# Layer 1's output mix applied to 128 middle features, and layers 1 and 2 skewed by a block in shared pools

## The chip, the cores and the metric

The kernel runs on one core of a Trainium2 chip, all in fp32. Its five engines work side by side, each in the order of its own instruction list: TensorE (PE in the profile, with its weight loads as PEld), VectorE (DVE), ScalarE (ACT), GpSimd (POOL), and SyncE (SP), which here only issues DMAs. The metric is the device time of one execution in microseconds; lower is better.

## The reference

Four graph layers over x of 128 x 64 x 256 (batch, node, feature), each in the form x = x + layer(relu(layernorm(x))):

```python
# layer 0: mix with a normalised adjacency, linear, batch norm, relu, linear, batch norm
# layer 1: spectral; U are the eigenvectors of the normalised Laplacian of adj
agg = jnp.einsum('mn,bnd->bmd', U.T, features)      # 256 features
h = jax.nn.relu(agg @ W1 + b1)                      # 128 features
out = h @ W2 + b2                                   # 256 features
return jnp.einsum('nm,bmd->bnd', U, out)
# layer 2: two adjacency layers, then LSTMs over windows of 1 to 4 nodes
h = jax.nn.relu(jnp.einsum('ts,bsh->bth', adj, x @ Wg0 + bg0))
h = jax.nn.relu(jnp.einsum('ts,bsh->bth', adj, h @ Wg1 + bg1))
...
# layer 3: edge attention over 512 edges
```

The eigenvectors U are computed on the chip, from a tridiagonal form made by Householder steps.

## The kernel before

The rows (128 x 64 = 8192) are cut into NB = 16 blocks of BT = 512 rows; a block X[i] is a resident tile of 128 partitions x TPB = 4 x D = 256. Two graphs of 64 nodes share the 128 partitions, so a mix over nodes is a matmul with a 128 x 128 block-diagonal matrix: BDU and BDUT for U and its transpose, BDA for the adjacency.

The program has these stages in order. `eigenvectors` computes U together with layer 0: a planner (`Plan`) lays layer 0's matmuls between the steps of the eigenvector chain and writes the order out by hand. A value is then loaded into a register and a branch (`self.tc.If`) holds a slower eigenvector method for the case that the fast one fails. `block_diagonal` makes BDA, BDU and BDUT after the branch. `layer1` follows, then `adjacency_layers`, the LSTM `windows`, and `layer3`. Outside the planned part the order on each engine is that of a scheduler that fills in by priority and readiness.

`layer1` for block i: `end0` (ACT applies layer 0's last batch norm to the stored `big` tiles, TensorE transposes them, VectorE adds them to X), `norm` (bn_stats, bn_aggr and a square root by steps, tiles n_st, n_mv, n_v, n_y, n_r, n_m; then ACT writes `h`), `mix` with BDU into `a`, W1 into PSUM, ACT's ReLU with bias b1 into `z`, W2 into PSUM, VectorE's addition of b2 into `y`, BDUT on y, and VectorE's addition to X. `adjacency_layers` first makes its tables (row sums w2_rs, B0, N0, b1) from ones, AT and the biases, then for each block runs norm, mix with BDA, W0, a max with the table N0 (`g`), W1, addition of b1 (`y`), and a second mix whose ReLU goes to `big` through ACT. In block 2 it also makes layer 3's tables from the list of edges (`edges`), in PSUM buffers of its own. Each of the two layers has pools of its own, opened with waits on what was in their place before.

DMAs go out on SP's queue in program order: the two adjacencies, 16 loads of X, layer 0's weights, the small vectors, then the rows of the Householder steps (`f_V<-f_x`, line 1046). Layer 1's weights are loaded inside `layer1`, after the branch, and layer 2's inside `adjacency_layers`.

Every matmul, VectorE and ACT instruction is recorded through one helper (`Ordered.call`), so all of them have line L799 in the profile and are told apart by their tiles; TensorE's `ps<-a,w` is W1 of layer 1 or W0 of layer 2, `pt<-w,z` or `pt<-z,w` is W2, `pt<-y,BDUT` the output mix, `pt<-ident,big` end0's transposes.

Of the kernel before, what the change touches and what calls it, by code (L numbers as in the profile page):

```python
# [8 lines left out]
F32 = mybir.dt.float32  # L9
# [885 lines left out]
class Fast:  # L895
# [197 lines left out]
    def reflectors(self):  # L1093
# [16 lines left out]
        for k in range(6):  # L1110
            p = self.mm((NT[:], B[:]))
            B2 = t(f"B{k + 1}", 64, 64)
            o.tt(B2[:], B[:], p[:], ALU.add if k else ALU.subtract)
            B = B2
            if k < 5:
                N2, NT2 = t(f"N{k + 1}", 64, 64), t(f"NT{k + 1}", 64, 64)
                self.act(N2[:], self.mm((NT[:], N[:]))[:], AF.Copy)
                self.act(NT2[:], self.mm((N[:], NT[:]))[:], AF.Copy)
                N, NT = N2, NT2
# [70 lines left out]
    def values(self):  # L1190
# [35 lines left out]
        X1 = t("X1", 128, 64)  # L1226
# [4 lines left out]
        F = t("F", 64, 64)  # L1231
# [124 lines left out]
    def verdict(self, U):  # L1356
# [4 lines left out]
        row, r2 = t("k_row", 64, 64), t("k_r2", 64, 64)  # L1361
# [63 lines left out]
P = 128  # L1425
# [21 lines left out]
class Kernel:  # L1447
# [57 lines left out]
    def block_diagonal(self, name, M, psum):  # L1505

        nc = self.nc
        bd = self.c(name, P, P)
        nc.vector.memset(bd[:], 0.0)
        p = psum.tile([P, N], F32, name="adj_ps")  # L1510
        self.mm(p[:], self.I2[:], M)
        self.o.copy(bd[0:64, 0:64], p[0:64, :])
        self.o.copy(bd[64:128, 64:128], p[64:128, :])
        return bd

    def adjacency(self, fast, plan):
# [9 lines left out]
        self.BDH = self.c("BDH", P, P)  # L1526
        nc.vector.memset(self.BDH[:], 0.0)
        rs, cs, dg, deg, junk = t("rs", 1), t("cs", 1), t("dg", 1), t("deg", 2), t("junk", N)
# [50 lines left out]
    def eigenvectors(self):  # L1579
# [3 lines left out]
        with ExitStack() as ex:  # L1583
# [12 lines left out]
            plan.emit()  # L1596
            bad = nc.values_load(left[0:1, 0:1], min_val=0, max_val=64)
# [5 lines left out]
        with ExitStack() as cx:  # L1603
            psum = cx.enter_context(self.tc.tile_pool(name="adjps", bufs=2, space=PSUM))
            self.BDA = self.block_diagonal("BDA", self.AT[:], psum)
            self.BDU = self.block_diagonal("BDU", self.U[:], psum)
            self.BDUT = self.block_diagonal("BDUT", self.UT[:], psum)
# [10 lines left out]
    def norm(self, pool, i, h=None):  # L1618
# [3 lines left out]
        if h is None:  # L1622
            h = pool.tile([P, TPB, D], F32, name="h")
        st = pool.tile([P, TPB, 6], F32, name="n_st")
        mv = pool.tile([P, TPB, 2], F32, name="n_mv")
        v, r, m = (pool.tile([P, TPB], F32, name="n_" + x) for x in "vrm")
# [5 lines left out]
        self.rsqrt(pool, r[:], v[:], "n")  # L1632
        o.stt(m[:], mv[:, :, 0], -1.0, r[:], ALU.mult, ALU.mult)
        for j in range(TPB):
            self.act(h[:, j, :], X[:, j, :], AF.Relu, scale=r[:, j:j + 1], bias=m[:, j:j + 1])
# [253 lines left out]
    def end0(self, i, psum):  # L1889

        sc2, sh2 = self.affine2
        for oc in range(2):
            self.act(self.part(i, oc), self.part(i, oc), AF.Identity, scale=sc2[:, oc:oc + 1], bias=sh2[:, oc:oc + 1])
        self.add_transposed(psum, i, lambda dc, j: self.part(i, dc)[:, j * P:(j + 1) * P])
# [3 lines left out]
    def layer1(self):  # L1898
        o, io = self.o, self.io
        cx, (w, pool, psum, ps2, ps0) = self.stage([("l1w", 1), ("l1", 2), ("l1ps", 3), ("l1bps", 3), ("l1eps", 2)])  # L1900
        with cx:
            W1 = self.weights(w, "w1_1", io["L1_gnn_W1"])
            W2 = self.weights(w, "w1_2", io["L1_gnn_W2"])
            b1 = self.columns(w, "w1_b1", io["L1_gnn_b1"])
            b2 = self.everywhere(w, "w1_b2", io["L1_gnn_b2"])

            self.end0(0, ps0)
            self.end0(1, ps0)
            hs = {0: self.norm(pool, 0)}
            for i in range(NB):  # L1910
                if i + 2 < NB:
                    self.end0(i + 2, ps0)
                if i + 1 < NB:
                    hs[i + 1] = self.norm(pool, i + 1)
                h = hs.pop(i)
                a = pool.tile([P, 2, BT], F32, name="a")
                self.mix(psum, h, self.BDU, lambda dc, p: self.move(a[:, dc, :], p[:]))
                p = psum.tile([P, BT], F32, name="ps")
                for kc in range(2):
                    self.mm(p[:], W1[:, kc, :], a[:, kc, :], kc == 0, kc == 1)  # L1920
                z = pool.tile([P, BT], F32, name="z")
                self.act(z[:], p[:], AF.Relu, bias=b1[:, 0:1])
                for jj in range(0, TPB, 2):
                    p = ps2.tile([P, 2, D], F32, name="pt")
                    for j in range(2):
                        self.mm(p[:, j, :], z[:, (jj + j) * P:(jj + j + 1) * P], W2[:, 0, :])
                    y = pool.tile([P, 2, D], F32, name="y")
                    o.add(y[:], p[:], b2[:, None, :].to_broadcast([P, 2, D]))
                    p = ps2.tile([P, 2, D], F32, name="pt")
                    self.mm(p[:].rearrange("p a b -> p (a b)"), self.BDUT[:], y[:].rearrange("p a b -> p (a b)"))  # L1930
                    x = self.X[i][:, jj:jj + 2, :]
                    o.add(x, x, p[:])
# [3 lines left out]
    def layer2(self):  # L1936
        self.adjacency_layers()
        self.windows()

    def adjacency_layers(self):  # L1940
        nc, o, io = self.nc, self.o, self.io
        cx, (w, pool, psum, ps2) = self.stage([("l2w", 1), ("l2", 2), ("l2ps", 4), ("l2bps", 2)])
        with cx:
            W0 = self.weights(w, "w2_0", io["L2_gnn_Wg0"])
            W1 = self.weights(w, "w2_1", io["L2_gnn_Wg1"])
            b0 = w.tile([1, D], F32, name="w2_b0")
            nc.sync.dma_start(b0[:], io["L2_gnn_bg0"][None, :])
            b1 = self.everywhere(w, "w2_b1", io["L2_gnn_bg1"])


            rs = w.tile([1, P], F32, name="w2_rs")
# [4 lines left out]
            B0, N0 = w.tile([P, 2, P], F32, name="w2_B"), w.tile([P, 2, N], F32, name="w2_N")  # L1956
# [9 lines left out]
            for i in range(NB):  # L1966
                if i == 2:
                    with ExitStack() as ce:
                        epool = ce.enter_context(self.tc.tile_pool(name="l3e", bufs=1, side="right"))
                        epsum = ce.enter_context(self.tc.tile_pool(name="l3eps", bufs=1, space=PSUM))  # L1970
                        nc.vector.hold, nc.scalar.hold, nc.tensor.hold = nc.vector.last, nc.scalar.last, nc.tensor.last
                        self.edges(self.w3, epool, epsum)
                        nc.vector.hold = nc.scalar.hold = nc.tensor.hold = None
                h = self.norm(pool, i)
                nc.sync.dma_start(self.spilled(i), self.X[i][:])
                a = pool.tile([P, 2, BT], F32, name="a")
                self.mix(psum, h, self.BDA, lambda dc, p: self.move(a[:, dc, :], p[:]))
                g = pool.tile([P, 2, BT], F32, name="g")
                for hc in range(2):
                    p = psum.tile([P, BT], F32, name="ps")  # L1980
                    for kc in range(2):
                        self.mm(p[:], W0[:, kc, hc * P:(hc + 1) * P], a[:, kc, :], kc == 0, kc == 1)
                    o.tt(g[:, hc, :].rearrange("p (b n) -> p b n", n=N), p[:].rearrange("p (b n) -> p b n", n=N),
                         N0[:, hc, None, :].to_broadcast([P, BT // N, N]), ALU.max)
                y = pool.tile([P, TPB, D], F32, name="y")
                for jj in range(0, TPB, 2):
                    p = ps2.tile([P, 2, D], F32, name="pt")
                    for j in range(2):
                        for kc in range(2):
                            self.mm(p[:, j, :], g[:, kc, (jj + j) * P:(jj + j + 1) * P], W1[:, kc, :],  # L1990
                                    kc == 0, kc == 1)
                    o.add(y[:, jj:jj + 2, :], p[:], b1[:, None, :].to_broadcast([P, 2, D]))
                v = self.nodes(i // 4)
                b = 8 * (i % 4)
                self.mix(psum, y, self.BDA, lambda dc, p: self.act(
                    v[:, dc, :, b:b + 8].rearrange("p n b -> p b n"), p[:].rearrange("p (b n) -> p b n", n=N), AF.Relu))
# [188 lines left out]
    def edges(self, w, pool, psum):  # L2185
# [28 lines left out]
        ps = [psum.tile([P, E], F32, name=f"ps{x}") for x in range(2)]  # L2214
# [12 lines left out]
        self.OS, self.OD = (pool.tile([P, E], F32, name="ed_" + n) for n in ("OS", "OD"))  # L2227
# [5 lines left out]
        for a, y in ((self.OS, self.OST), (self.OD, self.ODT)):  # L2233
            p = psum.tile([P, 4, N], F32, name="ps0")
# [10 lines left out]
        p = psum.tile([P, E], F32, name="ps1")  # L2245
# [3 lines left out]
        p = psum.tile([P, E], F32, name="ps0")  # L2249
# [201 lines left out]
    def run(self):  # L2451
# [4 lines left out]
        with cx:  # L2456
            self.big = [pool.tile([P, 2, 4 * BT], F32, name="big") for pool in pools]
            self.eigenvectors()
            self.layer1()
# [46 lines left out]
```

## Time and profile before

| | before |
|---|---|
| median of 3 runs | 2392.77 us (2391.76 to 2393.52) |
| profiled execution | 2392.81 us, of which the span is 2391.0 |
| mean granted TensorE clock | 0.989 |
| layer 0 and eigenvectors | 0 to about 382 us |
| branch | 382 to 388.9 us |
| layer 1 | 388.9 to 532.7 us |
| adjacency layers of layer 2 | 532.7 to 730.9 us |
| LSTM windows, then layer 3 | 730.9 to the end |

The profile gives, for each engine, the time that it was busy; a matmul in fp32 appears as two records. Records of TensorE overlap (their ends are modelled), so the distance between starts, and not the duration, is what one costs in a row. A window's row gives the busy time of PE, PEld, DVE, ACT and POOL in a stretch, each with its count, then the granted clock, the share of the DMA engines and what they moved. In a timeline or a group, the bracket or the last column is the idle time before the instruction and what ended it.

### The profile page before, as it was taken

The page shows a single profiled execution, that of the slowest core. Times are in us where ns is not written, and L with a number is a line of the kernel's source. Part 1 is how long each engine was busy: PE and PEld are TensorE (multiplying, and loading weights), DVE is VectorE, ACT ScalarE, POOL GpSimd, SP SyncE. Part 2 cuts the span into 40 slices and gives each one's busy share as a digit, 9 for nine tenths or more (in the row PEclk, how much of TensorE's full clock was granted, in tenths as well). Part 3 has the DMA queues.
Part 4 walks back from the last instruction along what each step waited for, and adds up shares of the span by engine and source line. Part 5 has one row for each costly group of instructions (what it writes and reads, how often), then busy time and mean ns, then how long its engine had stood idle before and what let it go on. Part 6 is the DMA issues. An engine that isn't in the chain of part 4 may idle for free.

```text
span 2391.0 us, 31925 instructions
## 1 busy us (share of the span) xinstructions
PE 2306.4 (96%) x11801; PEld 1601.0 (67%) x11801; DVE 1601.8 (67%) x4044; ACT 1137.3 (48%) x2488; POOL 2.5 (0%) x23
## 2 busy tenths in 40 slices
PE   5997998989999999999999999999999999999989
PEld 3554444656777778888999999888884444444434
DVE  6887675877536776677776677559755565656467
ACT  4675767434435663444444444335536544434321
POOL 0000000000000000000000000000000000000000
PEclk9999998999999999999999999999999999999989
DMA  5000211221001000000100002000011000000001
GB/s 159 1 1 1 71 54 33 69 82 36 1 1 36 1 18 1 1 1 1 36 1 1 1 1 71 1 1 16 1 34 38 1 5 18 14 14 18 14 14 49
DMA packets 61048, 54.77 MB, mean 23 GB/s; under 512 B 15188, under 2 KB 58709, under 8 KB 60885
## 3 DMA queue, kind: packets, MB, share of 16 engines
q1 hardware_dynamic: 60884, 52.66, 7.1%
q8 instruction: 95, 1.56, 0.3%
q14 instruction: 69, 0.56, 0.1%
HBM read 35.86 MB, written 16.78 MB: 22 GB/s over the span
## 4 chain that ended last, share of the span: by engine, by line
PE 78%; DVE 4%; ACT 1%; issue 1%; ACTq 0%; DVEq 0%
PE ps L799 67%; PE pt L799 5%; PE acc L799 5%; DVE sm_m L799 1%; PE y L799 1%; DVE X L799 1%; DVE aw L799 0%; DVE n_st L799 0%; ACT ls_g L799 0%; DVE g L799 0%; ACT big L799 0%; DVE sm_e L799 0%; DVE ls_g L799 0%; DVE y L799 0%; DVE n_mv L799 0%
## 5 line engine op out<-in xcount | busy, mean ns | idle before, releaser
L799 ACT ACTIVATE ls_g<-ls_g,ls_b 128x512 f32<-128x512 f32 (+4 forms) x472 | 243.0, 565 | 154.6 <-DVE ls_g L799 152.8
L799 ACT ACTIVATE ls_g<-ps,ls_b 128x256 f32<-128x256 f32 (+3 forms) x268 | 115.4, 470 | 329.4 <-PE ps L799 325.4
L799 PE MATMUL ps<-z,w 128*128 128x512 f32 x512 | 255.6, 625 | 0.0
L799 PE MATMUL ps<-big,X 128*128 128x176 f32 (+3 forms) x848 | 212.8, 366 | 1.1 <-ACT ls_z L799 1.0
L799 DVE TENSOR_TENSOR aw<-at,ed_OST 128x1024 f32<-128x1024 f32 x128 | 149.9, 1220 | 92.2 <-PE ps L799 92.2
L799 DVE TENSOR_TENSOR ls_g<-ls_z,ps 128x512 f32<-128x512 f32 (+5 forms) x256 | 146.9, 579 | 91.5 <-PE ps L799 90.0
L799 PE MATMUL ps<-ls_tx,X 128*128 128x160 f32 (+2 forms) x960 | 206.7, 326 | 1.2 <-DVE X L799 0.6
L799 PE MATMUL ps<-X,X 128*128 128x160 f32 (+1 forms) x896 | 199.0, 306 | 0.0
L799 PE MATMUL ps<-X,ls_w 128*128 128x256 f32 x640 | 190.5, 379 | 0.0
L799 PEld LDWEIGHTS ps<-ls_tx,X 128*128 128x128 f32 x960 | 161.8, 190 | 15.9 <-DVE X L799 5.5
L799 PEld LDWEIGHTS ps<-big,X 128*128 128x128 f32 x848 | 145.9, 190 | 31.0 <-issue 19.4
L799 DVE TENSOR_TENSOR X<-ls_g 128x1024 f32<-128x1024 f32 (+2 forms) x108 | 117.4, 1087 | 50.7 <-ACT ls_g L799 50.7
L799 ACT ACTIVATE r<-ps 128x512 f32<-128x512 f32 x256 | 129.4, 622 | 41.8 <-PE ps L799 41.7
L799 PEld LDWEIGHTS ps<-X,X 128*128 128x128 f32 x896 | 148.5, 190 | 0.0
L799 PE MATMUL ps<-X,ls_s 128*128 128x256 f32 x480 | 142.3, 379 | 0.0
L799 PEld LDWEIGHTS ps<-z,w 128*128 128x128 f32 x512 | 89.0, 192 | 72.8 <-issue 64.4
L799 PE MATMUL ps<-ls_tx,ls_s 128*128 128x256 f32 x464 | 134.8, 379 | 0.0
L799 PE MATMUL ps<-ls_tx,ls_w 128*128 128x256 f32 x464 | 133.3, 380 | 0.0
L799 PEld LDWEIGHTS ps<-X,ls_w 128*128 128x128 f32 x640 | 121.4, 190 | 16.8 <-DVE X L799 0.3
L799 PE MATMUL ps<-big,ls_w 128*128 128x256 f32 x464 | 131.9, 379 | 0.7 <-ACT ls_z L799 0.7
L799 PE MATMUL ps<-ed_S,Q 64*128 64x512 f32 x512 | 128.5, 617 | 1.4 <-DVE XV L799 1.3
L799 ACT ACTIVATE big<-ps 128x512 f32<-128x512 f32 x96 | 69.2, 755 | 124.2 <-PE ps L799 123.8
(524 smaller groups left out, 4029.5 us busy)
## 6 DMA issues: line engine op xcount, KB each, us to landing
X<-in_x_dram SPq DMA_DIRECT2D x32, 512.0 KB
xs<-X SPq DMA_DIRECT2D x16, 512.0 KB
X<-xs SPq DMA_DIRECT2D x16, 512.0 KB
out_dram<-X SPq DMA_DIRECT2D x32, 256.0 KB
X<-in_L_gnn_Wih_t_dram SPq DMA_DIRECT2D x4, 512.0 KB
ls_w<-in_L_gnn_Wih_t_dram SPq DMA_DIRECT2D x4, 512.0 KB
ls_w<-in_L_gnn_Whh_t_dram SPq DMA_DIRECT2D x4, 512.0 KB
w<-in_L_gnn_W_t_dram SPq DMA_DIRECT2D x2, 512.0 KB
```

Source lines behind the costliest of these rows:

```text
L799: i = method(*a, **kw)
```

## The change

- Layer 1's output mix moves ahead of W2. Since the mix acts on nodes and W2 on features, U(hW2 + b2) is (Uh)W2 plus a table; so BDUT is applied to the 128 features of h. For that, `first` leaves h with rows on partitions (a is the stationary operand, eight matmuls of 128 columns), the bias is taken out of the ReLU, max(p, -b1) on VectorE with the broadcast table N1, and what it leaves, with b2, is folded into the table T once, in iteration 1. The result of W2 plus T goes to `y`, and one addition of 1024 columns adds it to X.
- The blocks of layers 1 and 2 are skewed: layer 1 runs first(i), second(i-1), mixed_again(i), mixed(i+1), end0(i+3), norm(i+2); layer 2 runs W0 of i, the second mix of i-1, the first mix of i+1, W1 of i, norm(i+2). Both layers share one set of pools; layer 2's tables are made in iteration 4 of layer 1 and its first norm and mix are placed in layer 1's last block. The edge tables use the shared PSUM pool "pe".
- The block diagonals, the end of layer 0 for blocks 0 and 1 and the factors of block 0's norm stand ahead of the branch in the program; BDU and BDUT are made again inside the branch.
- Layer 1's weights are loaded at the start of the kernel, ahead of layer 0's.
- Some tiles of the eigenvector method are shared under one name, three memsets go to GpSimd, and the temporaries of the norm's square root are named apart.

```diff
+            for bd, M in ((self.BDU, self.U), (self.BDUT, self.UT), (self.BDA, self.AT)):
+                self.block_diagonal(bd, M[:], self.ps0)
+            for i in range(2):
+                self.end0(i, self.ps0, "ps")
+            self.norm0 = self.factors(self.w0, 0, self.const)
             bad = nc.values_load(left[0:1, 0:1], min_val=0, max_val=64)
...
-        cx, (w, pool, psum, ps2, ps0) = self.stage([("l1w", 1), ("l1", 2), ("l1ps", 3), ("l1bps", 3), ("l1eps", 2)])
+        cx, (w, pool, psum, ps2, ps0) = self.stage([("l1w", 1), ("l1", 2), ("l1ps", 4), ("l1bps", 2), ("l1eps", 2)])
...
+        def first(i):
+            p = psum.tile([P, TPB, P], F32, name="ps")
+            a = as_.pop(i)
+            for j in range(TPB):
+                for kc in range(2):
+                    self.mm(p[:, j, :], a[:, kc, j * P:(j + 1) * P], W1[:, kc, :], kc == 0, kc == 1)
+            g = gs[i] = pool.tile([P, 2, BT], F32, name="g")
+            o.tt(g[:, 0, :].rearrange("p (t c) -> p t c", c=P), p[:], N1[:, None, :].to_broadcast([P, TPB, P]), ALU.max)
+
+        def mixed_again(i):
+            g = gs[i]
+            p = psum.tile([P, BT], F32, name="ps")
+            for j in range(TPB):
+                self.mm(p[:, j * P:(j + 1) * P], g[:, 0, j * P:(j + 1) * P], self.BDUT[:])
+            self.act(g[:, 1, :], p[:], AF.Copy)
+
+        def second(i):
+            g = gs.pop(i)
+            y = pool.tile([P, TPB, D], F32, name="y")
+            for jj in range(0, TPB, 2):
+                p = ps2.tile([P, 2, D], F32, name="pt")
+                for j in range(2):
+                    self.mm(p[:, j, :], g[:, 1, (jj + j) * P:(jj + j + 1) * P], W2[:, 0, :])
+                o.add(y[:, jj:jj + 2, :], p[:], T[:, None, :].to_broadcast([P, 2, D]))
+            o.add(self.X[i][:], self.X[i][:], y[:])
+
+        mixed(0)
+        self.end0(2, ps0)
+        hs[1] = self.norm(pool, 1)
+        o.ts(N1[:], N1[:], -1.0, ALU.mult)
+        for i in range(NB + 1):
+            if i < NB:
+                first(i)
...
+            if i == 4:
+                tables()
+            if i:
+                second(i - 1)
+            if i < NB:
+                mixed_again(i)
+            if i + 1 < NB:
+                mixed(i + 1)
+            if i + 3 < NB:
+                self.end0(i + 3, ps0)
+            if i + 2 < NB:
+                hs[i + 2] = self.norm(pool, i + 2)
+            if i == NB - 1:
+                after()
...
+        def begin():
+            normed(0)
+            mixed(0)
+            normed(1)
+
+        def block(i):
+            if i == 2:
+                with ExitStack() as ce:
...
+            if i:
+                features(i - 1)
+            mixed(i + 1)
...
+            normed(i + 2)
...
+                self.weights1(ex.enter_context(self.tc.tile_pool(name="l1c", bufs=1)))
+                self.eigenvectors()
+                self.layers12()
+            self.windows()
```

## The prediction

> **What bounds the kernel now.** I read the page first (engine shares, slices, the chain that ended last), then the same kernel by windows over the stretch between the branch and the first LSTM window (382 to 731 us), which is all that the change rebuilds, then TensorE's timeline at its seams, and last the groups of instructions of layer 1.
>
> ```profile
> span 2391.0 us, 31925 instructions
> PE 2306.4 (96%) x11801; PEld 1601.0 (67%) x11801; DVE 1601.8 (67%) x4044; ACT 1137.3 (48%) x2488; POOL 2.5 (0%) x23
> ...
> PE   5997998989999999999999999999999999999989
> DVE  6887675877536776677776677559755565656467
> ...
> PE 78%; DVE 4%; ACT 1%; issue 1%; ACTq 0%; DVEq 0%
> ```
>
> TensorE is busy 96% and holds 78% of the chain, so a saved matmul is saved time wherever nothing else takes over. Busy shares hide the seams, so I go to windows (columns: length, then busy time of PE, PEld, DVE, ACT, POOL with counts, granted clock, DMA share, GB/s):
>
> ```profile
> 395.00:398.00 3.00, 1.84 (x12) 1.21 (x12) 3.00 (x14) 3.00 (x6) 0.00 (x0) 1.00 0.01 3
> 402.40:404.70 2.30, 2.30 (x12) 2.30 (x11) 1.65 (x6) 1.14 (x3) 0.00 (x0) 0.50 0.00 0
> ...
> 453.50:469.74 16.24, 16.21 (x81) 11.26 (x80) 14.48 (x45) 6.90 (x14) 0.00 (x0) 1.00 0.19 65
> ...
> 539.10:541.00 1.90, 1.90 (x10) 1.88 (x9) 1.48 (x9) 0.70 (x4) 0.00 (x0) 0.50 0.16 22
> ```
>
> The third row is two steady blocks of layer 1: TensorE full (8.11 us a block), VectorE already 14.48 of 16.24. The last row is the start of layer 2: matmuls at half clock. TensorE's timeline there (start, duration, operation, count, idle before it and its releaser):
>
> ```profile
> 468.02 1.02 PE L799 MATMUL pt<-y,BDUT 128*128 128x512 f32 x2
> 468.88 1.02 PE L799 MATMUL ps<-a,w 128*128 128x512 f32 x2
> ...
> 530.79 1.12 PE L799 MATMUL pt<-y,BDUT 128*128 128x512 f32 x2 [0.78 <-DVE y L799]
> 532.76 0.38 PE L799 MATMUL ps<-AT,ones 64*1 64x64 f32 x4 [0.85 <-DVE X L799]
> 535.54 1.19 PE L799 MATMUL ps<-w_rs,w_b 1*128 1x128 f32 x4 [2.40 <-DVE n_r L799]
> 537.25 2.07 PE L799 MATMUL ps<-w,w_B 128*128 128x256 f32 x4 [0.52 <-DVE w_B L799]
> 539.12 2.98 PE L799 MATMUL ps<-BDA,h 128*128 128x128 f32 x16
> 542.65 2.84 PE L799 MATMUL ps<-a,w 128*128 128x512 f32 x6 [0.56 <-DVE a L799]
> ```
>
> One logical fp32 matmul is two records. The first two lines give its pitch at 512 columns, 0.86; 256 columns cost 0.43, 128 columns 0.22, a transpose 0.13. The rest is the serial end of layer 1, the tables of layer 2 made one after another, and a first mix of 2.98 that costs 1.78 at full clock.
>
> **The change part by part.**
>
> (a) Layer 1's matmuls. Per block before: mix 1.78, W1 two of 512 columns 1.72, W2 1.84, BDUT two of 512 1.72, eight transposes 1.05: 8.11. After: mix 1.78, `first` eight of 128 columns 1.78, `mixed_again` four of 128 0.89, W2 1.84, transposes 1.05: 7.34. That is 0.77 less, 12.3 over 16 blocks, if TensorE stays the bound.
>
> (b) Layer 1's VectorE. The ReLU leaves ACT (`z<-ps`, 685 ns) and becomes a max on VectorE; two adds from PSUM become one SBUF add of 1024 wide. Rows:
>
> ```profile
> L799 DVE TENSOR_TENSOR X<-X,pt 128x512 f32<-128x512 f32 x63 | 42.6, 679 | 16.7 <-PE pt L799 15.8
> L799 DVE BATCH_NORM_STATS2 n_st<-X 128x6 f32<-128x256 f32 x64 | 25.1, 416 | 0.3
> ...
> 22.13 0.17 DVE L799 TENSOR_TENSOR m_m<-m_st 128x16 f32<-128x16 f32 x1
> 22.22 0.16 DVE L799 TENSOR_TENSOR m_d<-m_d 128x16 f32<-128x16 f32 x1
> ```
>
> Durations: six 512-wide operations (two `X<-X,pe`, `g`, two `y`, and `a`) at 0.68 are 4.08, the 1024-wide add 1.22 (the group aw<-at,ed_OST), four bn_stats 1.66, aggregation 0.36, seven small norm steps 1.15: 8.5 us a block, above today's 8.11. The Trainium skill, "VectorE: DVE Perf Modes", section "The DRAIN you can't avoid", says the next operation does not start until the pipeline is empty; taken literally that 8.5 is the period and layer 1 gets 6 us slower. The trace disagrees: the last two lines start 0.09 apart at 0.16 and 0.17 long, bn_stats follow each other at 0.33, 512-wide operations at 0.60; and today's operations have durations of about 8.0 a block in 7.24 busy. By these starts after is 6×0.60 + 1.14 + 4×0.33 + 0.36 + 7×(0.09 to 0.20) = 7.1 to 7.8. I use the starts. So VectorE comes level with TensorE. Period: 7.34 if TensorE wins, 7.8 if small steps stay dependent; I take 7.6, since two engines at equal load wait for each other in turn. 16×(7.6−8.11) = **−8**, ends −12 and −4.
>
> (c) Skew in layer 1. `second(i−1)`, 1.84 us, now stands between `first(i)` and `mixed_again(i)` on TensorE, and hides the 0.69 of `g`; without this cover each block would pay about 0.9. At the end, 16 steady blocks from the first mix at 400.35 would be over at 530.1, but the last BDUT matmul ends at about 531.9, after waits of 0.78 for y: **−2** (0 to −3.5).
>
> (d) Layer 2's tables go into iteration 4 and its first norm, first mix and second norm into the last block. From 531.9 to 542.65 are 10.75 us; 1.78 of mix stays, 1.2 of table matmuls come back at full clock, and the tables' VectorE work (5.5 busy from 532.7 to 539.1) falls on an engine with little room; I charge 2 of it. −10.75+1.8+1.2+2 = **−6** (−3 to −8). The four layer 2 weight and bias loads no longer follow layer 1; with their own pool they land inside it. Spilling X for layer 2's first blocks remains a store that nobody near waits for.
>
> (e) Skew in layer 2. A steady block takes 11.0 to 11.3 where its matmuls are 10.43; the excess is `pt<-w,g` waiting for g, `BDA,y` for y and the next mix for h. After, 3.6 us of mixes stand between W0 and W1. Over 16 blocks that is some 10, plus a wait of 1.2 at 599.6 after the edge tables; the edges still fill VectorE (16.8 of 20 us from 563 to 583) and their four table matrices now share two PSUM buffers with a rotating tag. I take **−7** (−2 to −11).
>
> (f) LSTM start. The bias loads `ls_b` stand on SP's queue behind a pool that now comes free early; 1.6 us of idle near 745 becomes about 0.3: **−1.5** (0 to −2).
>
> (g) "First norm in front of the branch". By the built order of instructions, batch-norm steps, the affine of the first blocks and their norm still follow the branch on all three engines; only the block diagonals and an ACT square come before it. ACT now does 18 `big` affines before its first `h` instead of 15, three of 0.72 more, against transposes that are then already done (60 against 36 before the first mix): **+1** for a later start (−1 to +3). On the clock, the Trainium skill ("TensorE: Matmul & The Clock Gate", Part 4) says transposes don't count as busy. That speaks against more transposes up front. The trace differs: clock 1.00 from 395 to 398 with only transposes issued, and 0.50 from 402.4 after a 2.04 us wait. The rule would add up to 1.7; I add **+1** because the waiting stretch ahead of the first mix remains.
>
> (h) Kernel start. Five layer-1 weight loads (450 KB) now stand on SP ahead of layer 0's weights and of the Householder rows.
>
> ```profile
> 34.08 0.27 DVE L799 SCALAR_TENSOR_TENSOR f_x<-f_uk,f_v,f_z 64x59 f32<-64x59 f32 x1 [6.66 <-DMA f_V<-f_x]
> ```
>
> VectorE already loses 6.66 here because the first row store is issued only at 32.11. At the measured 353 GB/s, 450 KB is 1.3 us; issues of 0.6 each would make it 3.0. The `N1` negation, hoisted into this chain just ahead of the same wait, needs a load issued at about 25 and is covered. **+1.5** (+0.5 to +3.5). The eigenvector chain carries this to the branch.
>
> (i) Eigenvector tiles reused, memsets on POOL, renamed norm temporaries in layer 3: their covers are the Householder waits for ACT and a full TensorE. 0 (−1 to +1). TensorE's order in the LSTM and layer 3 is unchanged.
>
> Sum: −8 −2 −6 −7 −1.5 +1 +1 +1.5 = **−21**. The profiled execution took 2392.81 (span 2391.0 plus 1.8 around it), level with the median 2392.77. Forecast **2371.8**.
>
> **The rivals.**
>
> *VectorE becomes layer 1's bound.* For: 7.8 by starts with dependent small steps, and the tables on top. Against: interleaved steps start 0.09 apart. It would give (a, b) −3, (c) 0, (d) −3, the rest unchanged: −12, so 2381.
>
> *Layer 2's skew hides little*, because the waits move to PSUM buffers or to the edges. For: VectorE 16.8 of 20 there. Against: 12.52 of 22.32 in steady blocks. (e) falls to −1: 2377.
>
> *TensorE keeps its place everywhere*: period 7.35, (e) −10: 2363.
>
> *Slower: g arrives late.* VectorE works in order, and `g(i)` stands behind `X<-X,pe` and bn_stats of block i+3. If these are held by ACT's affine or a transpose, `mixed_again(i)` waits on TensorE, then `a`, then `first(i+1)`. It needs more than 1.84 us of lateness to show, and, as the other parts give 13, a period above 8.11+0.81 = 8.92 to lose. Price at 9.4: 16×1.29−13 = +8, so 2400. Against it: ACT has 6.90 busy in 16.24 and is nowhere late in this layer.
>
> *The norm ahead of the branch really overlaps it.* The built order excludes it, as (g) says.
>
> **How the numbers follow.** Forecast case 50%, VectorE bound 20%, layer 2 unhelped 13%, full gain 12%, slower 5%. The likeliest case spans 2366 to 2377; VectorE-bound reaches 2385, the full gain 2361. Range 2361 to 2384. A measurement of this kernel can tell about 0.2%, 4.8 us, from no change: all cases but the last lie beyond it; a bad VectorE-bound case with a costly start could fall within. Faster 0.93, same 0.02, slower 0.05.
>
> **What would show it.** In the profile after: a steady layer 1 block of 7.4 to 7.8 with VectorE above 0.93 of it (a period of 7.35 with no VectorE wait on TensorE, or one over 7.9, says (b) is wrong); no idle TensorE or half clock between the layers; layer 2 blocks at 10.4 to 10.6; the wait at f_V ending near 35.6; first `ps<-BDU,h` at 402 to 404; LSTM start 20 to 23 us earlier. If the time is above 2385, a step of (b) to (e) has failed; below 2361, VectorE's load was overrated.

## The result and the profile after

The changed kernel takes 2361.43 us (median of 4 runs, 2361.14 to 2362.61) against 2393.14 of the kernel before beside it (2391.76 to 2393.69): a ratio of 0.9869, 95% interval 0.9852 to 0.9886, 31.7 us less. The forecast was 2371.8, 21 less, with a range from 2361 to 2384: the direction and the places were right, the size fell 0.4 us inside the lower end.

The page of the changed kernel, in the lines that answer to those shown of before:

```profile
span 2359.5 us, 32444 instructions
PE 2281.3 (97%) x12061; PEld 1618.5 (69%) x12061; DVE 1603.2 (68%) x4045; ACT 1134.5 (48%) x2488; POOL 2.9 (0%) x26
...
PE   5998997999999999999999999999999999999989
DVE  5887675999437786666777676559655566556467
...
PE 78%; DVE 3%; ACT 1%; issue 1%; DMA 0%; ACTq 0%; DVEq 0%
```

TensorE has 260 matmul records more and is busy 25 us less: more but shorter matmuls. In the VectorE row three slices of 9 have appeared, two over layer 1 and one over layer 2's first blocks. The same stretches as windows (two blocks in the middle of layer 1, two of layer 2):

```profile
464.86:479.31 14.45, 14.45 (x114) 13.98 (x113) 14.12 (x45) 6.70 (x15) 0.00 (x0) 1.00 0.21 71
...
601.56:622.48 20.92, 20.92 (x115) 16.28 (x113) 10.57 (x36) 9.44 (x16) 0.00 (x0) 1.00 0.00 1
```

TensorE is busy in every moment of both, at full clock; in layer 1 VectorE has 14.12 of 14.45 beside it. TensorE's timeline of the block just before that window and of the seam between the layers:

```profile
457.80 1.95 PE L799 MATMUL ps<-w,a 128*128 128x128 f32 x16
459.58 1.89 PE L799 MATMUL pt<-w,g 128*128 128x256 f32 x8
461.31 1.05 PE L799 MATMUL ps<-BDUT,g 128*128 128x128 f32 x8
462.20 1.95 PE L799 MATMUL ps<-BDU,h 128*128 128x128 f32 x16
463.99 1.04 PE L799 MATMUL pe<-ident,big 128*128 128x128 f32 x8
464.86 1.95 PE L799 MATMUL ps<-w,a 128*128 128x128 f32 x16
...
518.55 1.16 PE L799 MATMUL ps<-BDUT,g 128*128 128x128 f32 x8
519.55 1.06 PE L799 MATMUL ps<-BDA,h 128*128 128x128 f32 x8
520.46 0.70 PE L799 MATMUL pt<-w,g 128*128 128x256 f32 x2
521.00 1.15 PE L799 MATMUL ps<-BDA,h 128*128 128x128 f32 x8
521.98 1.46 PE L799 MATMUL pt<-w,g 128*128 128x256 f32 x6
523.28 3.60 PE L799 MATMUL ps<-a,w 128*128 128x512 f32 x8
```

By the starts, this block is 7.06 us: 1.78 for `first`, 1.73 for `second`, 0.89 for `mixed_again`, 1.79 for the next mix, 0.87 for eight transposes in a row. Not every block is like it. In the first three (409.17 to 428.11) ACT is busy 18.68 of 18.94 us, the fifth (435.03 to 444.32) carries layer 2's tables and takes 9.29, and from 469 us on single transposes stand between the matmuls of the mix and a block takes 7.2 to 7.9: the window above has 14.45 for two. The six blocks that start with the eighth to the thirteenth W1 are the fairest stretch to compare, in the changed kernel:

```profile
457.80:502.05 44.25, 44.25 (x341) 42.22 (x340) 42.28 (x127) 19.96 (x42) 0.00 (x0) 1.00 0.22 75
```

That is 7.38 a block, for 8.10 in the kernel before (459.06 to 507.68).

The seam has no bracket: layer 2's first mix runs between the halves of layer 1's last W2.

The way from one kernel to the other, between points that both have (U's matmul against the identity, layer 1's first mix, layer 2's first W0, the first LSTM matmul, the end of the span):

| stretch | before, us | after, us | difference | forecast |
|---|---|---|---|---|
| start to U's matmul | 382.55 | 384.24 | +1.7 | +1.5 (h) |
| to layer 1's first mix | 17.80 | 22.26 | +4.5 | +2 (g) |
| to layer 2's first W0 | 142.30 | 116.78 | -25.5 | -16 (a to d) |
| to the first LSTM matmul | 188.23 | 177.72 | -10.5 | -7 (e) |
| to the end | 1660.12 | 1658.50 | -1.6 | -1.5 (f) |
| span | 2391.0 | 2359.5 | -31.5 | -21 |

### The profile page after: what moved, and what is told of

It is laid out like the page before. It is cut to its first block, busy times and chain, and to the rows that moved or that the text cites. A ratio compares the mean times of both kernels' runs of the same rounds, so it can differ in the third digit from the quotient of the medians.

```text
span 2359.5 us, 32444 instructions
## 1 busy us (share of the span) xinstructions
PE 2281.3 (97%) x12061; PEld 1618.5 (69%) x12061; DVE 1603.2 (68%) x4045; ACT 1134.5 (48%) x2488; POOL 2.9 (0%) x26
## 4 chain that ended last, share of the span: by engine, by line
PE 78%; DVE 3%; ACT 1%; issue 1%; DMA 0%; ACTq 0%; DVEq 0%
PE ps L799 68%; PE acc L799 5%; PE pt L799 4%; PE y L799 1%; PE pe L799 1%; DVE sm_m L799 1%; DVE X L799 1%; ACT ls_g L799 0%; ACT big L799 0%; DVE aw L799 0%; ACT L799 0%; DVE n_st L799 0%; DMA ls_w<-in_L_gnn_Wih_t_dram 0%; ACT h L799 0%; DVE sm_e L799 0%
```

## The experiments

Each is the changed kernel (2361.43 us) with one edit. Repeats of code that is the same in several of these kernels put U's matmul anywhere from 383.3 to 385.1 us, so a difference of 2 us or less in the time is read from the stretches of the table and not from the total.

**e3: layer 1 without its skew.**

```diff
-            if i:
-                second(i - 1)
             if i < NB:
                 mixed_again(i)
+                second(i)
```

> The changed kernel, but in layer 1 second(i) follows mixed_again(i) in the same block and not a block later. Theory (second(i-1) is the cover of g; without it TensorE waits 0.5 to 0.9 a block): +8 to +14, 2370 to 2375 us. Rival (the scheduler puts transposes and the next mix there, so the cover is not needed): within 2 us of 2361.4.

Measured: 2374.81 us, +13.4. Its steady blocks start at 457.81, 465.90 and 474.05: 8.1 us, as in the kernel before. TensorE's waits from 440 to 520 us:

```profile
PE ps L799 <- DVE g L799: 4.6, 7, 0.8
PE ps L799 <- ACT a L799: 2.4, 5, 0.5
```

A block further on, in which no transposes are left, takes as long (506.34 to 514.37):

```profile
506.34 0.39 PE L799 MATMUL ps<-w,a 128*128 128x128 f32 x2
507.19 1.83 PE L799 MATMUL ps<-w,a 128*128 128x128 f32 x14 [0.46 <-ACT a L799]
509.80 1.16 PE L799 MATMUL ps<-BDUT,g 128*128 128x128 f32 x8 [0.78 <-DVE g L799]
...
514.37 0.39 PE L799 MATMUL ps<-w,a 128*128 128x128 f32 x2
```

So the period here is set by the way from `first` over g to the next matmul, and not by how much TensorE has to do. From the first mix to layer 2's first W0 e3 takes 132.62 us, 15.8 more than the changed kernel. The product order with fewer columns gains nothing by itself: what it takes from TensorE is given back in waiting.

**e2: the old order of the products, with the skew.**

```diff
-            for j in range(TPB):
-                for kc in range(2):
-                    self.mm(p[:, j, :], a[:, kc, j * P:(j + 1) * P], W1[:, kc, :], kc == 0, kc == 1)
...
+            for kc in range(2):
+                self.mm(p[:], W1[:, kc, :], a[:, kc, :], kc == 0, kc == 1)
...
+            self.act(g[:, 1, :], p[:], AF.Relu, bias=b1[:, 0:1])
...
+                self.mm(p[:].rearrange("p a b -> p (a b)"), self.BDUT[:], y[:, jj:jj + 2, :].rearrange("p a b -> p (a b)"))
...
+                o.add(x, x, p[:])
```

> The changed kernel with layer 1's products in the order of before (W1 with 512 columns, ReLU on ACT, W2, then the output mix over 256 features and two additions from PSUM), but with the skew, the shared pools, the tables in iteration 4 and everything else of the change. Theory (the middle-feature mix is worth its matmuls, 16 times 7.06 against 7.83 of TensorE): a steady block of 7.8 us, +12, 2373.5 us. Rival (most of layer 1's gain is the skew filling the stalls and the transposes in a row): period 7.5 or less, +7 or less, 2368 or less.

Measured: 2368.43 us, +7.0. The steady period is the 7.8 of the theory (460.58, 468.40, 476.22), but the sum is the rival's. From the first W1, seven blocks take 51.17 us here and 48.63 in the changed kernel: 2.5 less, and not seven times 0.76. Both wait there for some 1.5 us; but in the first three blocks ACT is nearly full in both (19.03 of 19.20 us here), which leaves a shorter TensorE little to gain. The next six take 46.93 for 44.25. With e3 these six give a square of mean periods: neither edit 8.10 (the kernel before, which lacks the rest of the change too), skew alone 7.82, product order alone 8.08, both 7.38. The gain is in the pair.

**e4: layer 2 without its skew.**

```diff
-            if i:
-                features(i - 1)
-            mixed(i + 1)
             y = ys[i] = pool.tile([P, TPB, D], F32, name="y")
...
+            features(i)
+            mixed(i + 1)
             normed(i + 2)
```

> The changed kernel, but in layer 2 the second mix of a block follows W1 of the same block and the next first mix stands behind it, as before. Theory (the skew removes 0.6 to 0.8 us of waits in a block, 10 in all): 2371 us, block period 11.0. Rival (the waits came from the pools and PSUM buffers of before, not from the order): 2361 to 2364 us, period 10.5.

Measured: 2368.66 us, +7.2; from the first W0 to the LSTM 185.85 us against 177.72. The period of before is back, with the new pools: 11.02 to 11.23 us behind the edge tables, for 11.02 to 11.3 in the kernel before. This window is two of its blocks:

```profile
600.30:622.76 22.46, 22.21 (x114) 16.37 (x113) 11.67 (x40) 9.45 (x16) 0.00 (x0) 1.00 0.00 1
...
578.26 3.67 PE L799 MATMUL ps<-a,w 128*128 128x512 f32 x8 [1.24 <-DVE a L799]
```

TensorE shows one declared wait of more than 0.3 us, the 1.24 behind the edge tables, where the kernel before has 1.23. The other 0.6 a block lies in larger distances between matmuls (W1 3.66 us for 3.46, each mix 1.94 for 1.78), which the profile gives no releaser for. The order removes both, not the pools.

**e8: tables and layer 2's beginning behind layer 1 in the program; e10: layer 2 in pools of its own.**

```diff
+            tables()
+            for step in [first] + rest:
...
-            if i == 4:
-                tables()
...
-            if i == NB - 1:
-                after()
```

> The changed kernel, but layer 2's tables and its first norm and mix stand in the program behind the last block of layer 1 instead of in blocks 4 and 15; the scheduler may still fill them in. Theory (part d: the serial tables and the cold first mix cost 6 to 10 us at this seam, and the program order is what takes them out): +5 to +9, 2366 to 2370 us. Rival (sharing the pools is enough: with nothing to wait for at the seam, the scheduler places the tables early by itself): within 2 us of 2361.4.

Measured: 2359.14 us, 2.3 less than the changed kernel. From the first mix to W0 it takes 117.69 us, 0.9 more than that; the 2.3 are not of the seam (U's matmul is 1.0 earlier, and a wait of 1.52 at the LSTM's first matmul is missing). The scheduler lays the tables into layer 1's last blocks by itself. In e10 the pools are parted too:

```diff
+            self.layer1(pool, psum, ps2, ps0, None, None)
...
+        cx, (w, pool, psum, ps2, ps0) = self.stage([("l2w", 1), ("l2", 2), ("l2ps", 4), ("l2bps", 2), ("l2eps", 2)])
+        with cx:
+            self.mixes2(w, psum)()
```

> The changed kernel, but layer 2 has pools of its own again, opened behind layer 1: its weights, tables, first norm and mix can start only when layer 1 gives its memory back. Theory (with the tables merely placed later the scheduler already closed the seam, so it is the shared pools that take out the serial tables and the cold mix): the idle stretch between the layers returns, +6 to +10, 2367 to 2371 us. Rival (the new order of layer 2 hides that start, and pools matter little): within 3 us of 2361.4.

Measured: 2371.77 us, +10.3. TensorE's timeline at its seam, and the window over it:

```profile
519.00 1.99 PE L799 MATMUL pt<-w,g 128*128 128x256 f32 x8 [0.75 <-ACT g L799]
520.93 0.38 PE L799 MATMUL ps<-AT,ones 64*1 64x64 f32 x4
528.68 1.19 PE L799 MATMUL ps<-w_rs,w_b 1*128 1x128 f32 x4 [7.37 <-DVE n_st L799]
530.38 2.08 PE L799 MATMUL ps<-w,w_B 128*128 128x256 f32 x4 [0.52 <-DVE w_B L799]
532.25 2.59 PE L799 MATMUL ps<-BDA,h 128*128 128x128 f32 x16
...
528.00:533.00 5.00, 3.81 (x12) 3.18 (x13) 3.64 (x21) 1.96 (x6) 0.00 (x0) 0.50 0.85 263
```

A wait of 7.37, then 5 us at half clock (DMA share 0.85). The releaser named is the last by the profile, a step of the norm; but VectorE wrote w_rs at 523.19, and SP issued layer 2's weights at 523.44 and 525.93 and the bias w_b at 526.44, just after layer 1's last addition (523.06). In the changed kernel the same loads go out at 389 to 390 us. So the seam is a matter of memory: layer 2's loads can start only when their place is free. Against e8, which has the same order and shared pools, the way from U's matmul to W0 is 10.0 us longer (150.8 for 140.8). Sharing the pools is what the change does for the seam; where the lines stand matters little.

**e1: layer 1's weights behind layer 0's.**

```diff
-                self.weights1(ex.enter_context(self.tc.tile_pool(name="l1c", bufs=1)))
+                self.l1c = ex.enter_context(self.tc.tile_pool(name="l1c", bufs=1))
...
+            self.weights1(self.l1c)
             left = fast.vectors(self.U[:], self.UT[:])
...
+        self.nc.vector.hold = self.nc.vector.last
         o.ts(N1[:], N1[:], -1.0, ALU.mult)
+        self.nc.vector.hold = None
```

> The changed kernel with one edit: layer 1's five weight loads are issued on SP behind layer 0's weights and the first rows of the Householder steps (as far as the built order lets them), and the negation of N1 is kept in layer 1. Theory (the loads ahead of the first f_V store delay the eigenvector chain by 2.7 us, 34.08 to 36.78, and everything follows): 2358.7 us, f_x after the f_V wait at 34 us again, first mix of layer 1 near 403.8. Rival (the delay is absorbed before the branch, the later first mix comes from the branch region): 2361.4 unchanged.

Measured: 2355.88 us, 5.5 less. VectorE's timeline in the changed kernel, then in e1:

```profile
30.43 0.23 DVE L799 TENSOR_SCALAR w_n<-w_n 128x128 f32<-128x128 f32 x1 [3.08 <-DMA w_n<-in_L_gnn_b_dram]
30.58 0.26 DVE L799 SCALAR_TENSOR_TENSOR f_v<-f_x,f_h_c,f_uA 64x60 f32<-64x60 f32 x1
36.78 0.27 DVE L799 SCALAR_TENSOR_TENSOR f_x<-f_uk,f_v,f_z 64x59 f32<-64x59 f32 x1 [5.94 <-DMA f_V<-f_x]
...
34.09 0.27 DVE L799 SCALAR_TENSOR_TENSOR f_x<-f_uk,f_v,f_z 64x59 f32<-64x59 f32 x1 [6.42 <-DMA f_V<-f_x]
```

The row store is waited for in both; the negation's own 3.08 costs nothing, since the store comes later anyway. The 2.7 us stay whole: U's matmul and layer 1's first mix are each 2.9 earlier in e1. A further 0.8 is the wait at the LSTM's first matmul, 0.68 for 1.52; the remaining 1.8 lie behind it or outside this one profiled execution and were not traced to a place.

**e9: everything behind the branch again; e7: the first norm ahead of ACT's affines.** In e9 the block diagonals, `end0` of blocks 0 and 1 and the norm are written behind the branch as in the kernel before. In e7:

```diff
+        h0 = nc.scalar.last
...
+        def ended(i):
+            nc.scalar.hold = h0
+            self.end0(i, ps0)
+            nc.scalar.hold = None
...
-                self.end0(i + 3, ps0)
+                ended(i + 3)
```

> The changed kernel with everything that was put ahead of the branch put behind it as before: block diagonals, end0 of blocks 0 and 1, and the first norm. Theory (the move costs: 8.1 us from the U matmul to bn_sh against 6.1 before, and the first h 2.5 later): -1 to -3, 2358.5 to 2360.5. Rival (the block diagonals ahead of the branch save what they promised): +1 to +2.

> The changed kernel, but ACT's affines of blocks 2 and later (end0) are held behind the first norm's four h instructions, so that 4 and not 18 affines stand ahead of them. Theory (the first mix waits at 406.5 for ACT's queue): first mix near 399, but the 44 transposes that were done ahead of it (4.8 us) come back into the layer; net -1 to -3, 2358.5 to 2360.5. Rival (the work done ahead was worth as much as the wait, or ACT, now behind, holds later blocks): 2361 to 2365.

Measured: e9 2359.49 us (-1.9), e7 2360.65 (-0.8). The first mix comes 18.5 us after U's matmul in e9 and 17.8 in e7, for 22.3 in the changed kernel. But from U's matmul to layer 2's first W0 the three take 138.9, 140.4 and 139.0: what is won before the first mix is lost behind it, in transposes that had been done ahead. The move in front of the branch is worth nothing either way; the 1.9 of e9 lie elsewhere, within the scatter named above. e7 shows one thing more. Its first mix, then the changed kernel's:

```profile
402.12 3.98 PE L799 MATMUL ps<-BDU,h 128*128 128x128 f32 x16 [4.55 <-ACT h L799]
...
406.50 1.95 PE L799 MATMUL ps<-BDU,h 128*128 128x128 f32 x16
```

The windows over e7's mix, and over transposes ahead of the mix in the changed kernel:

```profile
402.10:406.00 3.90, 3.88 (x17) 3.88 (x18) 2.75 (x14) 3.65 (x7) 0.08 (x1) 0.50 0.51 73
...
398.20:402.50 4.30, 3.26 (x24) 2.48 (x24) 4.08 (x15) 4.30 (x9) 0.00 (x0) 1.00 0.01 2
```

In both kernels sixteen transposes at half clock come first (393 to 398 us). Where TensorE then waits for 4.55, the clock is still 0.50 and the mix costs double; where more transposes follow, the clock is 1.00 and stays there.

**e5 and e6: more and less work for VectorE in layer 1.**

```diff
             o.add(self.X[i][:], self.X[i][:], y[:])
+            o.tt(y[:, 0:2, :], y[:, 0:2, :], T[:, None, :].to_broadcast([P, 2, D]), ALU.max)
```

```diff
-            self.mix(psum, hs.pop(i), self.BDU, lambda dc, p: self.move(a[:, dc, :], p[:]))
+            self.mix(psum, hs.pop(i), self.BDU, lambda dc, p: self.act(a[:, dc, :], p[:], AF.Copy))
```

> The changed kernel with one more VectorE instruction in each block of layer 1: a 512-wide max of y with T after the addition to X, written into y, whose result nobody reads (about 0.6 us a block; the outputs stay the same). Theory (VectorE is level with TensorE in layer 1, 14.12 busy of 14.45 us): the period follows VectorE, 7.06 to about 7.55, and the time rises by 6 to 9 us to 2368 to 2370. Rival (VectorE's small steps have slack that its busy time hides; TensorE is alone the bound): at most +2, 2363.

> The changed kernel with both halves of layer 1's first mix copied out of PSUM by ACT, so that VectorE has 0.6 us a block less and ACT 0.6 more (of 3.3 busy of 7.1). Theory (TensorE bounds the steady blocks, VectorE only the first ones): -1 to -3, 2358.5 to 2360.5. Rival (VectorE costs nothing now): 2361.4 unchanged. If VectorE holds the layer all along: -5 or more.

Measured: e5 2362.72 us (+1.3), e6 2357.39 (-4.0). From U's matmul to layer 2's first W0: 143.7 in e5, 139.1 in e6, 139.0 in the changed kernel. The six blocks from the eighth W1 on, in e6:

```profile
460.16:502.56 42.40, 42.40 (x338) 41.16 (x337) 39.98 (x125) 23.77 (x48) 0.00 (x0) 1.00 0.21 72
```

They take 47.43 us in e5, 44.25 in the changed kernel and 42.40 in e6. So in these blocks VectorE does set the pace: 0.6 us a block more costs 0.53, and 0.6 less gains 0.31, down to TensorE's own 7.07. Over the layer this does not show in e6, since the work went to ACT, which is full in the first three blocks: they take 21.43 us there (ACT 21.21 busy) for 18.94. No run moved the copies in the later blocks alone. Of e5's 4.7, 2.1 is made up behind W0 in the profiled execution, 1.5 of it the wait at the LSTM's first matmul; of e6's 4.0, 1.5 is that wait and the rest is not in this stretch. So e5's total fell in its rival's band by what happened behind the layer, while the layer followed the theory at half its size; e6's total fell between its cases.

**Combinations.** Two or all three of e1, e6 and e9 in one kernel:

> The changed kernel with two of the single edits: weights of layer 1 loaded behind layer 0's, and both halves of its first mix copied by ACT. If the gains (5.5 and 4.0) add up: 2351.9 us. Against the run with all three edits it tells what the move ahead of the branch costs once VectorE has room: 1.9 if the cost lies at the branch, 0 if it lay in VectorE's queue behind it.

> The changed kernel with three of the single edits: weights of layer 1 loaded behind layer 0's, both halves of its first mix copied by ACT, and everything put ahead of the branch behind it again. If the single gains (5.5, 4.0 and 1.9) add up: 2350.0 us. If the later start and VectorE's relief fall on the same waits: 2352 to 2354.

Measured: b5 2355.40 us, b3 2354.28 us. The gains do not add up (9.5 would have been the sum of two, 11.4 of three; 6.0 and 7.2 came). From U's matmul to W0, b5 takes 138.3 us and b3 136.1, while e9 and e6 alone have 138.9 and 139.1: the earlier first mix seems to be worth something only where VectorE has room, though some 2 us between one execution of each is little to go by. Some of what does not add up is one wait counted twice: that at the LSTM's first matmul is shorter in e1, absent in e6, and back at 1.53 in b3. b3 is the fastest of all, 0.9839 of the kernel before (0.9822 to 0.9855), though the 1.1 between it and b5 are within what this study can tell.

## Why the prediction was right in kind and short in size

*(a, b) Layer 1: the term that was mis-sized.* The period of 7.6 was near for the blocks that it describes: 7.38 on average in six of them, 0.31 above the 7.07 that TensorE needs when VectorE has room (e6). So the 0.26 for two engines "in turn" did come there. TensorE's own sum of 7.34 was too high: eight transposes cost 0.87 and W2 1.73, where the prediction had 1.05 and 1.84 from the steady blocks of before. Why they cost more there was not settled; seven of those eight transposes stood in a row too. But most of the layer is not in such blocks, and 16 times one period is not what it took. By TensorE's starts, without declared waits, from the first mix to layer 2's first W0:

| | before, us | after, us | difference | forecast |
|---|---|---|---|---|
| layer 1's four products | 116.0 | 103.0 | -13.0 | -8.2 (a, b) |
| its transposes | 12.4 | 7.8 | -4.6 | none |
| tables, layer 2's first mix | 6.4 | 4.4 | -2.0 | with the waits -8 (c, d) |
| declared waits | 7.5 | 1.6 | -5.9 | |

So the 9.5 us by which this stretch was better are the products, which gave what (a) has before its charge (12.3), and the transposes: 60 of 128 are done ahead of the first mix and not 36. The prediction set those 24 against the later start, in the one figure of (g); at 0.11 each they are some 2.7 us of this stretch. The choice between the summed durations (8.5) and the starts (7.1 to 7.8) was right. The sentence of the Trainium skill that the prediction cites ("VectorE: DVE Perf Modes", "The DRAIN you can't avoid") is not the whole of that section, which goes on that an operation that is not held starts earlier. The trace agrees with that: 512-wide operations start 0.60 apart at a duration of 0.68 to 0.69, and many small steps start 0.06 to 0.09 ahead of the next operation.

*(c) The cover of g.* The 0.9 a block that would be paid without it is near what e3 shows, 15.8 from the first mix to W0, 13.4 in the total. The prediction named it as a condition, though, and did not see that it was the larger half: without it (a) is worth nothing.

*(c, d) The seam.* The last two rows of the table are -7.9 for a forecast of -8. The mechanism was only half right: it is the shared pools (e10), not the place of `tables()` (e8).

*(e) Layer 2's skew.* -10.5, inside its bounds of -2 to -11; to the end of layer 2's last matmul alone it is some -12. The forecast took off some 4 for the edges, which now cost TensorE no declared wait. Steady blocks are 10.46, as forecast.

*(f)* The stalls at 745 us went, 1.6, but a new one of 1.52 stands at the LSTM's first matmul. The trace names ACT's `big`, which in e6 ends later than that matmul begins, so it is another wait; it is in this kernel and in b3, shorter in e1 and e2, and absent in the others. What makes it was not settled.

*(g)* +4.5 for +2. The direction was right, ACT's queue of 18 affines (without it, in e7, it is +0.0). But 1.9 of the 4.5 stand before the first transpose already (9.1 us behind U's matmul for 7.2), and the norm's small steps also stand in VectorE's queue between additions that wait for transposes; the step counted neither. The 1 us for a cold clock was wrong: the clock is 1.00 from 397.6 us on. The net cost is about zero by e9 and e7, because the transposes done ahead are kept.

*(h)* +1.7 at U's matmul, 2.7 at the f_V wait for +1.5 within +0.5 to +3.5; the wait ended at 36.78, not 35.6. *(i)* From there to U's matmul it is 347.5 us for 348.5 before: 1.0 less for a forecast of 0 (-1 to +1), within the scatter.

*Rivals.* The number lies nearest to the rival in which TensorE keeps its place everywhere (2363, given 12%), but not for its reason: VectorE did bound some six blocks (e5, e6), at 7.38 and not at 7.8. Layer 2's gain is that rival's. The late g, the slower rival, is what e3 makes real: a period of 8.1, still below the 8.92 from which it would have lost. Two of the rivals' totals do not follow from their own terms: VectorE as the bound sums to -11, 2382, and TensorE in its place to -28, 2365.

*Signs.* The seam without idle time or half clock and layer 2's period came as named. The first mix at 406.5 (for 402 to 404) and the LSTM's start 29.9 us earlier (for 20 to 23) did not.

## What to carry to other kernels

Cutting matmul columns and delaying their consumer by a block are one edit in two halves; price them as a pair, since each alone gave 0 to 0.3 us a block here and both 0.7. Work that one engine hands to another helps only in the blocks where the other has room (e6). Between two stages, ask first when memory comes free, and only then where the lines stand. Loads that are wanted 380 us later do not belong ahead of a store that a serial chain waits for.

## What the runs showed of the hardware

Transposes alone kept TensorE's clock up: in the changed kernel it is 1.00 from 397.6 us on, though until 406.5 there is nothing but transposes (6.46 us busy of 8.30), and the mix behind them takes 1.95 us; behind an idle 4.55 (e7) the same mix at 0.50 takes 3.98.

A busy share near 100% told nothing of the bound: in e3 VectorE is busy 17.07 of 17.87 us (482.13 to 500), yet TensorE waits for g there, and VectorE itself sits idle for 1.46 before a g (509.05); in the changed kernel, at 14.12 of 14.45, it does hold the blocks, as adding and taking away 0.6 us of its work shows.

The same matmuls cost differently from start to start in the two kernels' blocks, 0.11 for 0.13 a transpose and 1.73 for 1.84 in W2, with no declared wait in either; the cause was not settled.
